# Two pairs of blocks by two levels in the feed-forward's first pass, a fourth block prepared in self-attention, and down prepared after gate and up

## The chip, the cores and the metric

One core of a Trainium2 chip runs the whole program. The metric is the device time of one execution in microseconds. Beside the times stands a profiled execution of the same program, from which every duration below is read.

## What is computed

A decoder layer in float32 on 16 batches of 128 rows and 1024 columns: self-attention with one head of 256, a linear cross-attention with eight heads of 64, and a gated feed-forward whose three weight matrices are stored as four-bit numbers with a scale and a zero for each group of 64.

```python
x = x + self_attention(layernorm(x), Wqkv, bqkv, Wo, bo)
x = x + cross_attention(layernorm(x), ctx, ctx, Wq, Wk, Wv, Wo, bo, g)
n = layernorm(x)
Wg, Wu, Wd = (dequantize(W_q, scale, zero) for each of gate, up, down)   # 2752x1024, 2752x1024, 1024x2752
h = silu(n @ Wg.T) * (n @ Wu.T)
x = x + h @ Wd.T
```

## The kernel before

**Products by seven instead of eight.** The feed-forward cuts each matrix product into 2x2 parts and makes it from seven products of sums and differences of the parts instead of eight (a scheme of the Strassen and Winograd kind). The numbers of the seven are 1 to 7. `GATE` gives their order in gate and up, `DOWN` in down and in the outer level. Products add into each other in PSUM: 6, 5 and 3 go on in the bank of 1, and 4 in that of 7, so a bank is read by another engine between two products that write it.

**Blocks.** The 2752 inner columns are cut into ten blocks of 2 x 128 and a last one (`RB`) of 2 x 96. The rows are cut into two passes of eight batches (`PASSES`); pass 0 is the first pass. In pass 0, `one_block` makes a block with one level: for gate and for up seven products of four matmuls, each 128x128 weights by 512 columns. A float32 matmul shows as two records in the profile, so a block has 2 x 7 x 4 x 2 = 112 records, on line 1087. `last_block` makes the last one. In pass 1, `two_levels` takes two blocks and gate and up together: seven outer products (`OUTERS`, in the order of `DOWN`), each made of seven inner products of four matmuls with 256 columns. A pair has 7 x 7 x 4 x 2 = 392 records, tile name `q`.

**What surrounds a product.** In `products`, ScalarE copies products 1, 7 and 6 out of PSUM (tile `k`), and `got` gives VectorE the readings after 2, 5, 4 and 3: in the gate half an addition and ScalarE's silu (tile `sg`), in the up half an addition and a multiplication (tile `h`). Product 3 writes the bank that `got((1, 1), ...)` has read after product 5; only product 4 lies between. In `two_levels`, VectorE makes the inner operands of the next outer product (`inner_right`, tile `ti`, four instructions of 128x512), GpSimd the inner weights (`inner_left`, tile `li`, four), and `got` adds the readings into `U`, `V` and `C` with one to three VectorE instructions each. After the outer products 2, 3, 7 and 4, `finish` has ScalarE take the silu and VectorE multiply twice (`h`). `soon_due` and `extra` are lists of such work that `do_extra` puts between the inner products. In pass 1 the operands that `KEPT` names are made once and kept for all five pairs.

**Weights.** `prepare` is a generator that turns four-bit weights into the seven operands of each matrix of a block: `load_raw` loads numbers and scales, VectorE makes float numbers (tile `pa`), combines them (tile `pc`), and SyncE stores seven tiles of 256 KB to DRAM. Each call of `next` is one step: first half of the matrix, second half, combinations; the matrix "r" of the last block has one step only. Loads run two halves ahead (one in self-attention). `EARLY` = 3 blocks of gate and up are prepared in self-attention, where the loop over the four groups of batches (t = 0 to 3) calls `next` six times in the middle of t = 1 and t = 2 and three times behind them. The rest is prepared beside the products of pass 0: `attention_done` builds the list of jobs once the last work of cross-attention is done, in block 0, and `beside`, called after each product, makes a step after nine of a block's fourteen products. Gate and up alternate in the list with down.

`load_weights` loads the operands back, two to a tile of the pool `cw`, four tiles ahead (`AHEAD`), in the order of `to_load`. Most transfers go through SyncE's queue, in program order where the code asks for it.

**Order.** `InOrder` wraps an engine and keeps its instructions in the order of the program; without it the scheduler may move an instruction. `tensor` and `vector` are such wrappers; `products` uses `nc.tensor` directly. Memory comes from pools that are opened and closed in stack order on a left and a right side; a tile waits for whatever lay there before.

**Before block 8** (`RB - 2`) the operands of pass 1 are loaded (`pass1`, eight transfers of 512 KB) into the pool `cxb`, which `attention_done` opens.

Of the kernel before, what the change touches and what calls it, by code (L numbers as in the profile page):

```python
# [18 lines left out]
P = 128  # L19
# [46 lines left out]
def decoder_layer(  # L66
# [215 lines left out]
    EARLY = 3  # L282
# [27 lines left out]
    with (  # L310
# [166 lines left out]
        for t in range(NT):  # L477
# [14 lines left out]
            for f in range(4):  # L492
# [9 lines left out]
                if more and t > 0:  # L502
                    for _ in range(1 + f % 2):
                        next(early, None)
# [457 lines left out]
    with ExitStack() as gs:  # L962
# [9 lines left out]
        def attention_done():  # L972

            nonlocal cxb, rest
            sides.close()
            prep_pools(second, "f", 6, 2)
            jobs = []
            for blk in range(EARLY, len(BLOCKS)):
                jobs += [(blk, mat) for mat in ("gu" if blk < RB else "rm")]
                if blk >= EARLY + 2:  # L980
                    jobs.append((blk - EARLY - 2, "d"))
            jobs += [(blk, "d") for blk in range(len(BLOCKS)) if (blk, "d") not in jobs]
            rest = prepare(jobs, 2, nc.sync, vector)
            banks.append(pool("c_u", 4, space=PSUM, side="right"))
            cxb = pool("c_xb", 1)
# [9 lines left out]
        def tiles_of(blk):  # L995
# [3 lines left out]
        OUTERS = [(i, q) for i in range(NI) for q in DOWN]  # L999
        to_load = deque(  # L1000
            [t for blk in range(len(BLOCKS)) for t in tiles_of(blk)]
            + [[(2 * i + f, mat, q) for mat in "gu"] for i, q in OUTERS for f in range(2)]
            + tiles_of(RB)
        )
# [65 lines left out]
        def products(T, got):  # L1070
# [7 lines left out]
            def product(q):  # L1078
# [7 lines left out]
                for j in range(JC):  # L1086
                    nc.tensor.matmul(  # L1087
# [20 lines left out]
        def one_block(blk, T, between):  # L1108
# [21 lines left out]
            make = {"g": products(T, gate), "u": products(T, up)}  # L1130
# [4 lines left out]
        def last_block(ps, T, between):  # L1135
# [24 lines left out]
            def half_product(p, w, q, start, stop):  # L1160
                for j in range(JC):
                    nc.tensor.matmul(  # L1162
# [63 lines left out]
        R = {}  # L1226

        def inner_right(T, q):

            if q in KEPT and (q, 7) in R:  # L1230
                return []

            def t(kc, h):
                return T[q][:, ts(kc, CHUNKS), ts(h, HT)]

            R[q, 1], R[q, 2], R[q, 3] = t(0, 0), t(1, 0), t(1, 1)

            def comb(k):
                if k == 5:
                    tag = KEPT.get(q, "ti")  # L1240
                    pool = {"ti": deep_pool, "X4": [xres]}.get(tag, [xlate])[0]
                    R[q] = pool.tile([P, 4, CHUNKS, HT], F32, name="ti", tag=tag, bufs=1)
                dst = R[q, k] = R[q][:, (5, 6, 7, 4).index(k)]
                a, b = {
                    5: (t(0, 1), t(0, 0)),
                    6: (t(1, 1), R.get((q, 5))),
                    7: (t(1, 1), t(0, 1)),
                    4: (t(1, 0), R.get((q, 6))),
                }[k]
                vector.tensor_tensor(dst, a, b, ALU.subtract)  # L1250

            return [lambda k=k: comb(k) for k in (5, 6, 7, 4)]

        def inner_left(L, pool, tag):
# [9 lines left out]
            def comb(k):  # L1264
                t = L[k] = pool.tile([P, 2, CHUNKS, P], F32, name="li", tag=tag)
# [10 lines left out]
        deep_pool = []  # L1276
        deep = ExitStack()

        def two_levels(T):
            scalar = InOrder(tc, nc.scalar)  # L1280
            deep_pool.append(
                deep.enter_context(
                    tc.tile_pool(name="c_d", bufs=1, side="right", reuse_waits="tile")
                )
            )
# [14 lines left out]
            def multiply(n, p):  # L1300
# [5 lines left out]
                ps = bank[set_]  # L1306
                for m in range(2):
                    for c in range(CHUNKS):
                        tensor.matmul(
                            ps[:, m, :],  # L1310
# [7 lines left out]
                if p in (1, 7, 6):  # L1318
# [3 lines left out]
                    scalar.copy(t, ps)  # L1322
# [28 lines left out]
            def finish(i, q):  # L1351
# [5 lines left out]
                def mult(f):  # L1357
# [4 lines left out]
                    if s == 1:  # L1362
                        store(2 * i + f, 4, half, t)
# [20 lines left out]
            def prepare_outer(n):  # L1384
                state[n] = {"L": {}, "bank": {}, "kept": {}}

                state[n]["left"] = inner_left(
                    state[n]["L"], *((chc, "hc") if n == 0 else (ct, "sg"))
                )
# [6 lines left out]
            for n, (i, q) in enumerate(OUTERS):  # L1396
                last = n + 1 == len(OUTERS)
                if q in (1, 5):
                    sums["U" if q == 1 else "V"] = deep_pool[0].tile(
# [9 lines left out]
                if q not in (1, 5):  # L1409
                    sums["C"] = deep_pool[0].tile(wide, F32, name="C")  # L1410
                if not last:
                    soon_due.extend(inner_right(T, OUTERS[n + 1][1]))
                if n == 0:
                    extra.append(lambda: outer_operand(T, 4))
                elif n == 4:
                    extra.extend(inner_right(T, 4))
# [20 lines left out]
                load_weights()  # L1437
                if not last:
                    do_extra(len(soon_due))
                    multiply(n + 1, 7)  # L1440
                if q in (2, 3, 7, 4):
                    finish(i, q)


                if q == 3:
# [9 lines left out]
                del state[n]  # L1455
            return extra
# [10 lines left out]

        for n in range(AHEAD):
# [4 lines left out]
        T1 = {}  # L1473

        def beside(n, mat, q):
# [4 lines left out]
            elif n % 7 in (0, 2, 4, 5) or n == 6:  # L1480
                next(rest, None)

            if blk == RB:
                for k in {("r", 0): (5,), ("r", 1): (7,), ("m", 6): (6,)}.get((mat, q), ()):
                    outer_operand(T1, k)
                if (mat, q) == ("m", 1):
                    for step in inner_right(T1, 1):
                        step()

        for blk in range(len(BLOCKS)):  # L1490
            if blk == RB - 2:
# [4 lines left out]
            if blk == RB:  # L1496
                blocks.update(pass1)
                last_block(0, T, beside)
            else:
                one_block(blk, T, beside)  # L1500
# [4 lines left out]
        remaining = two_levels(T1)  # L1505
# [272 lines left out]
```

## Time and profile before

| | us |
|---|---|
| median of three runs | 2297.44 (2296.18 to 2297.61) |
| the profiled execution, its own time | 2296.27 |
| its span, first to last instruction | 2294.5 |
| block 0's first product to the first of block 1 (with the end of cross-attention) | 808 to about 884 |
| blocks 1 to 9 of pass 0 | about 884 to 1317 |
| two levels in pass 1, five pairs | 1355 to 1780 |
| down | from 1818 |

The rows come from the page's span and from the chain of work that ended last. A row of the chain gives a start, a length and what ran, with x for the count of records. A row of the table by stretches gives the busy time of each engine with its number of instructions, the granted clock of TensorE as a share of full speed, the mean busy share of the 16 DMA engines (a little over 1 when they are full) and the rate. A row of single instructions gives start, length, engine, line, operation and tiles (out<-in), and in brackets how long the engine had been idle and what ended that. PE is TensorE's matmuls, PEld its weight loads, DVE VectorE, ACT ScalarE, POOL GpSimd, SP SyncE. Line 62 is the wrapper's, so tiles tell such instructions apart.

### The profile page before, as it was taken

The page shows a single profiled execution, that of the slowest core. Times are in us where ns is not written, and L with a number is a line of the kernel's source. Part 1 is how long each engine was busy: PE and PEld are TensorE (multiplying, and loading weights), DVE is VectorE, ACT ScalarE, POOL GpSimd, SP SyncE. Part 2 cuts the span into 40 slices and gives each one's busy share as a digit, 9 for nine tenths or more (in the row PEclk, how much of TensorE's full clock was granted, in tenths as well). Part 3 has the DMA queues.
Part 4 walks back from the last instruction along what each step waited for, and adds up shares of the span by engine and source line. Part 5 has one row for each costly group of instructions (what it writes and reads, how often), then busy time and mean ns, then how long its engine had stood idle before and what let it go on. Part 6 is the DMA issues. An engine that isn't in the chain of part 4 may idle for free.

```text
span 2294.5 us, 25166 instructions
## 1 busy us (share of the span) xinstructions
PE 2269.7 (99%) x8928; PEld 1581.6 (69%) x8928; DVE 1554.0 (68%) x2210; ACT 555.4 (24%) x887; POOL 389.2 (17%) x283
## 2 busy tenths in 40 slices
PE   8999999999999999999999999999999999999999
PEld 7556566666666664444444468888888588888888
DVE  6694788788788836677776548777777655444463
ACT  2111256665665652111111111222121100000000
POOL 5120122222222210000000024444443000000000
PEclk9999999999999999999999999999999999999999
DMA  6242356566576657888789733654654974434631
GB/s 245 62 138 90 110 156 184 164 193 189 161 229 203 171 157 249 264 273 281 260 282 332 256 104 103 202 173 140 202 183 145 328 243 153 140 125 148 221 115 37
DMA packets 274797, 425.19 MB, mean 185 GB/s; under 512 B 26225, under 2 KB 119793, under 8 KB 274545
## 3 DMA queue, kind: packets, MB, share of 16 engines
q1 hardware_dynamic: 254192, 396.06, 54.5%
q10 hardware_dynamic: 18016, 18.62, 2.6%
q0 software_dynamic: 2464, 8.91, 1.0%
q8 instruction: 71, 1.16, 0.2%
q14 instruction: 54, 0.43, 0.1%
HBM read 265.62 MB, written 157.35 MB: 184 GB/s over the span
## 4 chain that ended last, share of the span: by engine, by line
PE 94%; DVE 3%; DMA 1%; issue 1%; ACT 0%; SPq 0%; POOL 0%; DVEq 0%; POOLq 0%; ACTq 0%
PE p L1087 23%; PE po L1663 21%; PE q L62 18%; PE mm L62 11%; PE kq L62 8%; PE mm L392 5%; PE tr L62 3%; PE mm L407 2%; PE mm L288 2%; PE p L1162 1%; PE tr L339 1%; DMA kh<-kd 1%; DVE bnst L62 0%; DVE qden L62 0%; DMA wo_again<-in_wo 0%
## 5 line engine op out<-in xcount | busy, mean ns | idle before, releaser
L1087 PE MATMUL p<-b,w 128*128 128x512 f32 x704 | 310.4, 592 | 0.7 <-DMA w<-wg 0.7
L1087 PEld LDWEIGHTS p<-b,w 128*128 128x128 f32 x704 | 133.4, 190 | 167.1 <-issue 162.8
L1087 PE MATMUL p<-T,w 128*128 128x512 f32 x528 | 234.2, 592 | 0.0
L62 PE MATMUL q<-ti,li 128*128 128x256 f32 x840 | 193.0, 379 | 1.0 <-DVE ti L62 1.0
L1087 PEld LDWEIGHTS p<-T,w 128*128 128x128 f32 x528 | 100.1, 190 | 124.6 <-issue 123.1
L1663 PE MATMUL po<-wc,lc 128*128 128x256 f32 x840 | 183.4, 379 | 0.0
L62 POOL TENSOR_TENSOR li<-w 128x512 f32<-128x512 f32 x70 | 96.1, 1374 | 514.6 <-DMA w<-wu 476.8
L62 PEld LDWEIGHTS q<-ti,li 128*128 128x128 f32 x840 | 159.2, 190 | 23.8 <-issue 1.7
L1663 PEld LDWEIGHTS po<-wc,lc 128*128 128x128 f32 x840 | 159.6, 190 | 21.8
L708 POOL TENSOR_TENSOR qe<-qe,qden 128x1024 f32<-128x1024 f32 x64 | 121.6, 1900 | 266.3 <-DVE qden L62 233.6
L62 ACT COPY k<-q 128x512 f32<-128x512 f32 x105 | 61.4, 585 | 324.8 <-PE q L62 324.8
L62 DVE TENSOR_TENSOR pa<-pa,sz 128x512 f32<-128x512 int32 (+1 forms) x172 | 129.0, 750 | 5.4
L1663 PE MATMUL po<-wq,lq 128*128 128x256 f32 x560 | 126.7, 379 | 0.0
L62 PE MATMUL mm<-kh,cxt 128*128 128x256 f32 x512 | 123.0, 383 | 3.3 <-DMA kh<-kd 3.1
L62 PE MATMUL kq<-cx,wk_sb 128*128 128x512 f32 x256 | 122.0, 599 | 3.5 <-ACT ke L665 3.5
L62 PEld LDWEIGHTS mm<-qs,m_sb 128*128 128x128 f32 x512 | 97.2, 190 | 38.9 <-issue 28.0
L62 PE MATMUL kq<-wq_sb,xn 128*128 128x512 f32 x256 | 120.4, 593 | 0.0
L62 PE MATMUL mm<-qs,m_sb 128*128 128x256 f32 x512 | 120.3, 379 | 0.0
L62 PEld LDWEIGHTS mm<-kh,cxt 128*128 128x128 f32 x512 | 96.1, 190 | 33.6 <-issue 18.5
L62 DVE TENSOR_REDUCE qmx<-kq 128x16 f32<-128x1024 f32 x64 | 76.3, 1193 | 63.0 <-PE kq L62 62.8
L1663 PEld LDWEIGHTS po<-wq,lq 128*128 128x128 f32 x560 | 106.0, 190 | 15.7 <-issue 0.9
L392 PE MATMUL mm<-xnT,wqkv_sb 128*128 128x512 f32 (+1 forms) x320 | 113.2, 510 | 0.0
(189 smaller groups left out, 3651.9 us busy)
## 6 DMA issues: line engine op xcount, KB each, us to landing
w<-wu SPq DMA_DIRECT2D x140, 256.0 KB, 3.5
lq<-h SPq DMA_DIRECT2D x140, 256.0 KB, 4.4
w<-wg SPq DMA_DIRECT2D x138, 256.0 KB, 3.0
kd<-kt SPq DMA_DIRECT2D x64, 512.0 KB, 3.5
kh<-kd SPq DMA_DIRECT2D x128, 256.0 KB, 5.6
h<-hc SPq DMA_DIRECT2D x80, 256.0 KB, 2.8
wq<-wd SPq DMA_DIRECT2D x70, 256.0 KB, 5.0
h<-h SPq DMA_DIRECT2D x60, 256.0 KB, 3.2
```

The source lines that it names most:

```text
L62: return lambda *args, **kw: self._tc.keep_in_program_order(fn(*args, **kw))
L288: tensor.matmul(ps, oT[:, d, ts(b % BPT, S)], wo_d[d][:, ts(h, 512)], start=(d == 0), stop=(d == 1),)
L339: nc.tensor.transpose(tr[:, j, :], xn[:, ts(4 * h + j, P)], ident)
L392: nc.tensor.matmul(ps[:, tokens], wqkv_sb[:, f, c, :], xnT[:, c, tokens], start=(c == 0), stop=(c == CC - 1),)
L407: nc.tensor.matmul(ps, xnT[:, c, ts(i, S)], wqkv_sb[:, 4:6, c, :], start=(c == 0), stop=(c == CC - 1),)
L708: nc.gpsimd.tensor_tensor(qe, qe, den.unsqueeze(2).to_broadcast(wide), ALU.mult)
L1087: nc.tensor.matmul(ps, wt[:, j, :], T[q][:, j, :], start=(first == q and j == 0), stop=(q in (2, 3, 4) and j == JC - 1), skip_group_check= ...
L1162: nc.tensor.matmul(bank[p], w[:, j, :], T[q][:, j, :], start=(start and j == 0), stop=(stop and j == JC - 1), skip_group_check=True,)
L1663: nc.tensor.matmul(bank[:, i, :], l[:, ts(i, S)], w,  start=(start and c == 0 and i % 2 == 0), stop=(stop and c == len(pairs) - 1), skip_g ...
```

## The change

- `EARLY` becomes 4, and the six calls of `next` are made in t = 3 too.
- The list of jobs for the rest has gate and up of blocks 4 to 9 first, then four blocks of down, the last block's "m" and "r", then the other seven of down.
- `PAIRS = [2, 3]`: blocks 4 to 7 are made in pass 0 by `two_levels(0, ...)`, between block 3 and block 8; `to_load` follows. With `ps == 0` the function stores both h of a block as `one_block` does, keeps no operands for later pairs, and takes its tiles from a pool `c_d` that is opened before block 3 and closed after the stage. The operands for its first outer product are made in block 3.
- `beside` makes a step after twelve of fourteen products of a block, after five in the last block; in the stage a step follows the outer products 1, 2 and 5.
- `cxb` is opened, and the operands of pass 1 are loaded, after the stage.
- `products` and `half_product` use the wrapper `tensor`, but for block 0.

```diff
-    EARLY = 3
+    EARLY = 4
...
-                if more and t > 0:
+                if t > 0:
                     for _ in range(1 + f % 2):
                         next(early, None)
...
             prep_pools(second, "f", 6, 2)
-            jobs = []
-            for blk in range(EARLY, len(BLOCKS)):
-                jobs += [(blk, mat) for mat in ("gu" if blk < RB else "rm")]
-                if blk >= EARLY + 2:
-                    jobs.append((blk - EARLY - 2, "d"))
-            jobs += [(blk, "d") for blk in range(len(BLOCKS)) if (blk, "d") not in jobs]
+            jobs = [(blk, mat) for blk in range(EARLY, RB) for mat in "gu"]
+            down = [(blk, "d") for blk in range(len(BLOCKS))]
+            jobs += down[:4] + [(RB, "m"), (RB, "r")] + down[4:]
             rest = prepare(jobs, 2, nc.sync, vector)
             banks.append(pool("c_u", 4, space=PSUM, side="right"))
-            cxb = pool("c_xb", 1)
...
+        PAIRS = [2, 3]
+        order = [blk for blk in range(RB) if blk // 2 not in PAIRS]
+        order.insert(2 * PAIRS[0], None)
+        to_load = deque([t for blk in order[: 2 * PAIRS[0]] for t in tiles_of(blk)])
+        to_load += [t for i in PAIRS for t in tiles_of_pair(i)]
+        to_load += [t for blk in order[2 * PAIRS[0] + 1 :] + [RB] for t in tiles_of(blk)]
+        to_load += [t for i in range(NI) for t in tiles_of_pair(i)] + tiles_of(RB)
...
-        def products(T, got):
+        def products(T, got, tensor=tensor):
...
-                    nc.tensor.matmul(
+                    tensor.matmul(
...
+            engine = nc.tensor if blk == 0 else tensor
+            make = {"g": products(T, gate, engine), "u": products(T, up, engine)}
...
+        class Operands:
+            def __init__(self, T, kept):
+                self.T, self.kept, self.R, self.pool = T, kept, {}, None
...
+                        R[q] = pool.tile(
+                            [P, 4, CHUNKS, HT],
+                            F32,
+                            name="ti",
+                            tag=tag,
+                            bufs=1 if self.kept else 2,
+                        )
...
-        def two_levels(T):
+        def two_levels(ps, pairs, operands, between=lambda q: None):
...
+                    if ps == 0:
+                        store(2 * i + f, 1 + s, half, t)
+                    elif s == 1:
                         store(2 * i + f, 4, half, t)
...
+                do_extra(len(soon_due))
                 if not last:
-                    do_extra(len(soon_due))
                     multiply(n + 1, 7)
                 if q in (2, 3, 7, 4):
                     finish(i, q)
+                between(q)
...
-            elif n % 7 in (0, 2, 4, 5) or n == 6:
+            elif n % 7 != 3 and (blk < RB or n % 2 == 0):
                 next(rest, None)
+            if blk == 2 * PAIRS[0] - 1 and n == 9:
+                for step in first_operands.inner_right(DOWN[0]):
+                    step()
...
-        for blk in range(len(BLOCKS)):
-            if blk == RB - 2:
+        for blk in order:
+            if blk is None:
+                two_levels(
+                    0, PAIRS, first_operands, lambda q: q in (1, 2, 5) and next(rest, None)
+                )
+                deep.close()
+                cxb = pool("c_xb", 1)
                 pass1 = new_blocks(cxb, lambda k: f"b{k}")
                 for _ in block_loads(1, pass1):
                     pass
```

## The prediction

> **What bounds the kernel now.** I read the page's busy shares first, then the chain that ended last, then stretches of the second half, and last single instructions of the two-level stage.
>
> ```profile
> PE 2269.7 (99%) x8928; PEld 1581.6 (69%) x8928; DVE 1554.0 (68%) x2210; ACT 555.4 (24%) x887; POOL 389.2 (17%) x283
> ```
>
> TensorE is busy for 99%, so time can only come from fewer or shorter matmuls, and any wait put in front of a matmul is paid in full. The chain in order of time (start, length, what) shows what a matmul costs when nothing holds it up:
>
> ```profile
> 874.31 439.47 PE p L1087 x1024
> 1436.14 343.87 PE q L62 x1592
> ```
>
> One 512-column record of a one-level product costs 439.47/1024 = 0.4292 us, one 256-column record of a two-level product 343.87/1592 = 0.2160 us. Blocks 1 to 9 of the first pass run without one gap (112 records, 48.07 us each; block 1 starts near 884.4, block 8 near 1221), and so do four of the five pairs of the second pass. The same stretches by engine (columns: stretch, length, busy PE, PEld, DVE, ACT, POOL with instructions, PE clock, DMA share, GB/s):
>
> ```profile
> 200.00:220.00 20.00, 20.00 (x52) 9.54 (x51) 0.00 (x0) 2.06 (x3) 0.00 (x0) 1.00 0.28 102
> ...
> 881.00:929.00 48.00, 48.00 (x113) 21.28 (x112) 34.80 (x59) 7.29 (x11) 0.00 (x0) 1.00 0.84 273
> ...
> 1249.60:1257.60 8.00, 8.00 (x20) 3.61 (x19) 5.23 (x10) 1.17 (x2) 0.00 (x0) 1.00 1.04 256
> 1257.60:1265.60 8.00, 8.00 (x20) 3.47 (x19) 7.76 (x13) 0.00 (x0) 0.00 (x0) 1.00 1.05 347
> ```
>
> The clock is full throughout. VectorE has room in a block (34.80 of 48), none of its work lies in 200 to 220, and in block 8 the DMA engines are already full: over the nine slices of 8 us from 1217.6 to 1289.6 they moved 315, 405, 349, 364, 256, 347, 311, 370 and 358 GB/s, 342 on average, at shares of 0.99 to 1.05.
>
> **What is removed: 896 records become 784 shorter ones.** Two pairs are four blocks: 4 x 112 x 0.4292 = 192.3 us go. By two levels a pair is 7 x 7 products of four matmuls of two records, 392: 2 x 392 x 0.2160 = 169.3 us come. **-22.9 us.** Everything below is what may be given back.
>
> **The fourth early block.** A gate or up matrix is 16 VectorE instructions. In the first pass six of them (one step) take 3.58 us from start to start, the four combinations 2.53: 2 x 3.58 + 2.53 = 9.7 us a matrix, three steps. Two more matrices are 19.4 us. The early calls now run into the last group of four batches: there VectorE is empty from 199.5 to 222.1, under 27.5 us of query and key products (191 to 218.6), the first slice above. The SyncE queue issues 4 raw loads, 4 scale loads and 14 stores more; behind them wait the context loads issued at 201.9, first used after 257, and the loads that it issues at 244.5. Cost 0; without that cover it would be up to 19.4. ACT and GpSimd are not touched there.
>
> **Blocks 1 to 3: twelve steps instead of nine.** VectorE: 28.6 us of preparation for three matrices (tiles pa and pc in that stretch) become 38.1, plus the block's own 6.2: 44.3 of 48.07. The place that can bite: product 3 adds into the bank that `got` reads after product 5, with only product 4 (3.43 us) between. After the reading that follows product 4 come, on VectorE, step, step, then three more: in steady state I find that reading 0 to 1 us late, so 2.4 us are in hand. DMA: four matrices of 2.62 MB (4 raw or scale loads, 7 stores of 0.262), 3.67 of weights, 1.05 of h: 15.2 MB, and 15.7 with the 0.5 by which the measured stretch (13.1) exceeds its count: 327 GB/s against 342. Between 0 and 4 us; I take 1, as the same waits cost nothing at 273.
>
> **The two-level stage itself.** Its VectorE work: the page's forms on C, U, V and h sum to 229.1 us for five pairs, 45.8 a pair; combinations of operands are made anew each time, 28 x 0.78 (ti) = 21.8; three steps 9.7. That is 77.3 of 84.7 us. In the second pass most ti are kept, so its first pair shows the tight spot (start, length, engine, what):
>
> ```profile
> 1393.55 1.75 DVE L62 TENSOR_TENSOR ti<-T,ti 128x512 f32<-128x512 f32 x1
> ```
>
> ```profile
> 1393.12 1.64 POOL L62 TENSOR_TENSOR li<-w,li 128x512 f32<-128x512 f32 x1 [3.89 <-PE q L62]
> ```
>
> ```profile
> 1393.78 3.69 PE L62 MATMUL q<-ti,li 128*128 128x256 f32 x16 [0.81 <-DVE ti L62]
> ```
>
> After outer product 2, VectorE must multiply h twice (2.4 us), then do two readings and three ti before inner product 7 of the next outer: TensorE lost 0.81 us. And a VectorE instruction with both inputs in SBUF that meets a GpSimd one waits for it: 1.75 for 0.69. The change puts a 3.6 us step ahead of those h, behind which wait both readings and the ti. VectorE idles there for 2.6 us until ACT's silu, so 1 to 2.3 us come on top: 1.7 to 3.1. The second tight outer is 7: three instructions per reading, two h and now four ti. Its products in the trace have the matmul at 1430.8; its last needed reading ended at 1433.2 with the h 0.9 us later than it need be and no ti. Three ti of 0.6 put it at 1434.1, 3.3 late; if no GpSimd instruction is met, 1.4. The step after 1 and the combinations after 5 find VectorE idle for 5.1 and 4.6 us: 0. So per pair 3.1 to 6.4 us; met collisions could double the larger spots (1.07 each). Two pairs: 3 (if the silu wait covers all of the step) to 16; I take 2 per tight outer, **+8**, nearer to the low rows since in the trace most meetings were harmless. GpSimd's 56 li (1.37 us, 77 us) and ACT's copies lie beside it, as they do in the second pass.
>
> [...]
>
> **Blocks 8 and 9, where down is now prepared.** 73 steps are left (12 matrices of gate and up x 3, 11 of down x 3, 3 for m, 1 for r). Block 0 takes 3 (in the trace its first step comes after the twelfth product), blocks 1 to 3 take 36, the stage 6: block 8 has steps 46 to 57, which are d3, m, r, d4 and most of d5, block 9 58 to 69, down alone, and the last block the rest. A down matrix moves 3.41 MB (scales are 0.52 a half). Block 8, with loads two units ahead: 5.9 of loads, 7.1 of stores, 3.67, 1.05, and 4.19 of the second pass's x: 21.9 MB. Block 9: 5.9 + 7.3 + 3.6 + 1.05 = 17.9. About 4.1 MB may still be on the way at the end of it (two units of loads, four stores, three weight tiles). (39.8 - 4.1)/0.342 = 104.4 us against 96.1: 8.3 late. VectorE is in order, so a raw tile that is late holds the readings behind it, and TensorE after the 3.4 us of product 4: **+5**. At the fastest slice (405) it is 0; at the two slices quoted (302 on average, those with most down scales) it is 18.7. Now the nine slices show VectorE waiting 4.3 us for DMA in all, and TensorE not at all, with nine steps. SyncE issues about 94 transfers in block 9 at 0.5 us each (60 us for some 120 in those slices), so that queue is full too. It costs the same lateness, not a second one.
>
> [...]
>
> **The rest.** Products held in program order: in blocks 1 to 9 the trace has them in that order already, 0. Two new changes of stage (0 to 2 us; the one in the trace, 1354.8, has no gap): +0.5. Five steps in the last block: VectorE is busy for 16.1 of 41 us there, 17 more fit, 0.
>
> **Sum** against the profiled execution (2296.27, of which the span is 2294.5): -22.9 + 1 + 8 + 5 + 0.5 = -8.4, 2287.9. The median shown is 1.2 higher: **2289**.
>
> **Rivals.** *(a) All of it is hidden but 3 us in the stage:* -20, 2277.5. For it: no gap in blocks 8 and 9 now, at full DMA. Against: those blocks carry a third more. 0.15. *(b) VectorE and GpSimd eat the gain in the stage:* 5 us per tight outer, 20 instead of 8: 2301, within what counts as no change. For it: 91% of VectorE's time taken before any collision. Against: the five pairs of the second pass lost 1.7 us in all (425.0 us from 1354.98 to 1780.01, for 1960 x 0.2160 = 423.4). 0.2. *(c) DMA turns blocks 8 and 9 slower:* at 302 GB/s 18.7 instead of 5: 2303. It decides below 316 GB/s: there 35.7 MB take 112.9 us, 13.4 more than 96.1 + 3.4, which is what the other terms leave. For it: the two slices. Against: the mean of nine. 0.2, with the worse forms of (b) in it. **Forecast as summed:** 0.45.
>
> Two in a thousand (4.6 us) is about what a measurement of this kernel can tell from no change. Faster by more (below 2292.8): forecast and (a), 0.6. Within: (b), 0.2. Slower: (c), 0.2. The range reaches from (a) to (c): 2278 to 2303; the forecast's own is 2283 to 2295.
>
> **What would show it.** 784 records of line 1087 and 2744 of q; blocks 8 and 9 longer than 48.07 with VectorE waiting for raw or szd; in the stage waits of q for ti after outers 2 and 7, and 169.3 us plus them; blocks 1 to 3 at 48.1; VectorE busy from 200 to 220 with no longer self-attention. A stage below 173 us, or blocks 8 and 9 without a gap, would make the terms wrong; so would a wait at a place that I have at 0.

## The result and the profile after

The changed kernel takes **2317.28 us** (median of 7 executions, 2305.64 to 2318.36) beside 2296.18 us for the kernel before (7 executions on the same chip, 2294.36 to 2297.61): a ratio of **1.0075, 95% interval 1.0054 to 1.0097**. It is 0.75% slower. The prediction was 2289 us, faster, in a range from 2278 to 2303; the result lies outside it, on the other side. The profiled execution took 2317.28 us, its span 2315.5, against 2296.27 and 2294.5 before.

The page of the changed kernel, busy times and two of the groups (busy time and mean ns, then the idle time in front of them and who ended it):

```profile
PE 2263.5 (98%) x9264; PEld 1653.1 (71%) x9264; DVE 1678.3 (72%) x2340; ACT 564.9 (24%) x899; POOL 469.1 (20%) x339
...
L62 PE MATMUL q<-ti,li 128*128 128x256 f32 x1176 | 281.4, 391 | 17.4 <-DVE ti L62 17.4
...
L62 PE MATMUL p<-b,w 128*128 128x512 f32 x432 | 193.0, 599 | 5.4 <-DVE h L62 5.4
```

The 336 records more (8928 to 9264) are the 448 of 0.4292 us that went and the 784 of 0.2160 that came, as the working of the first step had them, 4 x 112 and 392 x 2; the 896 in that step's heading is a slip that entered no sum. TensorE is still busy for 98%, but it now waits, and those records that it does run are longer in the mean (391 ns instead of 379, 599 instead of 592). The waits of the changed kernel from 880 to 1420 us, from block 1 to some way into the second pass (engine, who is waited for, us in total, times, longest):

```profile
PE q L62 <- DVE ti L62: 17.2, 9, 3.4
PE p L62 <- DVE h L62: 5.4, 2, 3.5
PE q L62 <- DVE C L62: 1.8, 1, 1.8
PE q L62 <- DVE U L62: 1.5, 1, 1.5
```

All of them end on VectorE; two of the nine on ti, 0.83 and 0.82 us, lie in the second pass. By stretches of the changed kernel (the new stage; block 8; block 9; the last block and what of block 9 was late; columns as in the prediction):

```profile
1032.30:1233.60 201.30, 182.47 (x786) 155.44 (x785) 168.99 (x209) 32.49 (x51) 73.44 (x52) 0.94 0.45 147
1233.60:1281.60 48.00, 48.00 (x113) 21.24 (x112) 39.90 (x68) 7.06 (x11) 0.00 (x0) 1.00 0.98 322
1281.60:1329.60 48.00, 44.82 (x105) 19.57 (x103) 39.08 (x66) 5.97 (x10) 0.00 (x0) 0.99 1.05 336
1329.60:1373.90 44.30, 43.97 (x96) 19.40 (x97) 38.94 (x55) 3.98 (x7) 1.76 (x2) 0.93 0.80 252
```

Three things stand in the first line. The stage took 201.3 us for 169.3 us of matmuls. VectorE was busy for 169.0 us of it: as much as TensorE's matmuls take at the full clock, so a stage of the length that was counted left it no room at all. And the granted clock was 0.94, where it had been 1.00 in every stretch of the kernel before that the prediction looked at. Block 8 lost nothing; block 9 lost its time at one wait and in the slow clock behind it.

Put together, against the kernel before (us, from the start of the first product to the end): the first product starts 1.5 later; blocks 1 to 3 take 2.1 more; the stage takes 201.27 where 784 x 0.2160 = 169.34 were counted, **+31.9**; blocks 8 and 9 with the last block 140.4 instead of 133.9, +6.5; the second pass's stage +1.1; down +0.8. That is 43.9 given back against 22.9 gained: +21.0, the difference of the two profiled executions.

**Where the 31.9 lie.** The waits in the stage sum to 18.8 us: in the first pair 1.54 (on U, outer product 1), 2.36 (on ti, after 2), 2.27 (after 6), 0.84 (after 3) and 3.43 (after 7), in the second 1.77 (on C, in 6), 2.36 (after 6), 0.84 (after 3) and 3.43 (after 7). "After 6" stands for the wait ahead of inner product 7 of the outer product that follows 6. Most of the other 13 us are matmuls that ran slowly. TensorE's own timeline (start, length, what, idle before):

```profile
1062.65 5.23 PE L62 MATMUL q<-ti,li 128*128 128x256 f32 x16 [2.36 <-DVE ti L62]
...
1092.63 3.62 PE L62 MATMUL q<-ti,li 128*128 128x256 f32 x16
...
1121.61 6.45 PE L62 MATMUL q<-ti,li 128*128 128x256 f32 x16 [3.43 <-DVE ti L62]
```

Sixteen such records take 3.62 us with no wait ahead of them, 5.23 after one of 2.36 and 6.45 after one of 3.43. The granted clock in stretches of 3.41 us around the last of these shows it (the clock is the third figure from the end):

```profile
1116.96:1120.37 3.41, 1.22 (x6) 0.74 (x4) 3.34 (x5) 0.00 (x0) 1.26 (x1) 1.00 0.12 44
1120.37:1123.79 3.42, 2.18 (x5) 1.85 (x6) 2.89 (x5) 0.00 (x0) 0.00 (x0) 0.50 0.00 0
1123.79:1127.20 3.41, 3.41 (x9) 2.70 (x8) 0.23 (x1) 1.54 (x2) 1.27 (x1) 0.50 0.00 0
1127.20:1130.61 3.41, 3.41 (x17) 2.97 (x16) 1.82 (x4) 0.59 (x1) 1.26 (x1) 1.00 0.43 159
```

TensorE was busy for 1.22 us of the first stretch; the clock is 0.50 in the whole of the next, again in the one after it, and back at 1.00 in the fourth. The stage has seven such stretches, block 9 two. A stretch of 3.41 us at half speed costs 1.71 us where TensorE is busy for all of it; less the idle time that falls into them, the seven cost 10.8 us. Some 2 us lie in the records beside the nine waits: a record lasts 0.38 us, though the next one of an unbroken row starts 0.2160 us after it, so a wait costs 0.16 us more than its idle time, and the first records behind it run a little longer.

**Why VectorE was late.** In the prediction a step takes 3.58 us. The first one in the stage, put after outer product 1 (VectorE and then GpSimd, both of the changed kernel):

```profile
1048.26 1.49 DVE L62 TENSOR_SCALAR pa<-raw 128x512 int32<-128x512 int32 x1
1049.77 2.37 DVE L62 TENSOR_TENSOR pa<-pa,szd 128x512 f32<-128x512 int32 x2
1052.06 1.49 DVE L62 TENSOR_SCALAR pa<-raw 128x512 int32<-128x512 int32 x1
1053.58 1.42 DVE L62 TENSOR_TENSOR pa<-pa,szd 128x512 f32<-128x512 int32 x2
...
1060.76 1.75 DVE L62 TENSOR_TENSOR ti<-T 128x512 f32<-128x512 f32 x1
```

```profile
1048.18 1.27 POOL L62 TENSOR_TENSOR li<-w,li 128x512 f32<-128x512 f32 x1 [5.21 <-PE q L62]
1049.92 3.35 POOL L62 TENSOR_TENSOR li<-w 128x512 f32<-128x512 f32 x2 [0.46 <-PE q L62]
...
1060.44 1.52 POOL L62 TENSOR_TENSOR li<-w,li 128x512 f32<-128x512 f32 x1 [4.01 <-PE q L62]
```

The step met three combinations of GpSimd: an instruction of 0.42 us took 1.49 twice, a pair of 1.42 took 2.37, and the step 6.7 us instead of 3.58. The next step began with the same instruction, with no GpSimd one beside it:

```profile
1063.63 0.41 DVE L62 TENSOR_SCALAR pa<-raw 128x512 int32<-128x512 int32 x1
```

In the whole stage 41 of VectorE's 209 instructions took over 0.2 us longer than the shortest of their kind, 38 us in all, and every one of them ran beside a GpSimd instruction; the 14 that read q out of PSUM beside one took no longer than the others of their kind, at most 0.69 us. Nothing waited for the first step at its place. But the readings of the next outer product's banks and its ti queue behind it on VectorE, one ti met GpSimd once more (1.75 for 0.68), and the matmuls that need it began 2.36 us late.

### The profile page after: what moved, and what is told of

Its sections match the earlier page's. It is cut to its first block, busy times and chain, and to the rows that moved or that the text cites. A ratio compares the mean times of both kernels' runs of the same rounds, so it can differ in the third digit from the quotient of the medians.

```text
span 2315.5 us, 26157 instructions
## 1 busy us (share of the span) xinstructions
PE 2263.5 (98%) x9264; PEld 1653.1 (71%) x9264; DVE 1678.3 (72%) x2340; ACT 564.9 (24%) x899; POOL 469.1 (20%) x339
## 5 line engine op out<-in xcount | busy, mean ns | idle before, releaser
L62 PE MATMUL q<-ti,li 128*128 128x256 f32 x1176 | 281.4, 391 | 17.4 <-DVE ti L62 17.4
L62 PEld LDWEIGHTS q<-ti,li 128*128 128x128 f32 x1176 | 230.0, 196 | 54.6 <-issue 13.2
L62 POOL TENSOR_TENSOR li<-w 128x512 f32<-128x512 f32 x98 | 135.2, 1381 | 374.2 <-DMA w<-wu 296.7
L62 ACT COPY k<-q 128x512 f32<-128x512 f32 x147 | 86.1, 585 | 499.6 <-PE q L62 499.6
L62 PE MATMUL p<-b,w 128*128 128x512 f32 x432 | 193.0, 599 | 5.4 <-DVE h L62 5.4
L62 PEld LDWEIGHTS p<-b,w 128*128 128x128 f32 x432 | 83.0, 193 | 110.2 <-issue 99.5
L62 PE MATMUL p<-T,w 128*128 128x512 f32 x304 | 134.7, 592 | 0.0
L62 PEld LDWEIGHTS p<-T,w 128*128 128x128 f32 x304 | 57.8, 190 | 72.7 <-issue 71.7
```

Source lines behind the costliest of these rows:

```text
L62: return lambda *args, **kw: self._tc.keep_in_program_order(fn(*args, **kw))
```

## The experiments

Two theories stood at the start. **V:** the stage loses its time because VectorE is late, and the clock falls because TensorE waits. **D:** the moved steps and their transfers cost time wherever they lie. Ratios are to the kernel before on the same chip, with 95% intervals. "The last three blocks" are 8, 9 and the last one, 133.91 us before. The length of a stage and its waits come from the one profiled execution of each kernel. In experiment 6 the changed stage, with the same nine waits, took 197.1 us instead of 201.3, as four stretches of half clock fell into it and not seven. So a difference of about 4 us between two stages says little.

**1. No steps in the stage.** The weights of down for blocks 1 and 2 are not prepared; those of block 0 take their place.

```
-            jobs += down[:4] + [(RB, "m"), (RB, "r")] + down[4:]
+            jobs += [down[0], down[3]] + [(RB, "m"), (RB, "r")] + down[4:]
...
-                    0, PAIRS, first_operands, lambda q: q in (1, 2, 5) and next(rest, None)
+                    0, PAIRS, first_operands, lambda q: None
```

> The changed kernel without the six preparation steps in the two-level stage of the first pass: down of blocks 1 and 2 is not prepared, and block 0's is used in its place. Everything else stands. Theory V (VectorE is late in the stage; TensorE waits 18.8 us there for ti, U and C, and the granted clock halves after the waits over 2 us, 13 us more): the waits in the outer products 1, 2 and 6 go (9 of 18.8 us), those in 3 and 7 stay (0.84 and 3.43 us, twice), so the stage falls from 201 us to about 185, the whole to about 2301. Theory D (twelve steps a block and the transfers moved with them cost the time, wherever they lie): the stage may shorten by a few us, the whole stays above 2312.

Measured: 2298.21 us, ratio 1.0005 (0.9995 to 1.0015). The stage took 185.2 us, as theory V had it. The waits after 2 and 6 are gone; the 1.55 on U, which the expectation had among those that go, 0.82 after 3 and 3.44 after 7 stay in place. So the six steps, 19.4 us of VectorE's work by the prediction's rows, cost some 16 of the stage's 31.9 us, and the steps are not all of it.

**2. No combinations of operands in the stage.** The four ti of the first outer product stand in for those of all others, 52 VectorE instructions fewer; the steps stay.

```
+                if not self.kept and (DOWN[0], 4) in R:
+                    for k in (5, 6, 7, 4):
+                        R[q, k] = R[DOWN[0], k]
+                    return []
```

> The changed kernel with the inner operands ti made for the first outer product of the stage alone; the other thirteen use the same tile, so 52 VectorE instructions are left out. The six steps stay. Theory V: no wait for ti is left and the readings are 2.4 us earlier in each outer product; the stage comes down from 201 us to 170 to 174, the clock stays full there, the whole is 2317 - 28 = about 2289, block 9 still losing its 6.5. Theory D: above 2310, since steps and transfers are unchanged.

Measured: 2286.95 us, ratio 0.996 (0.9945 to 0.9975), the stage 172.0 us. Its line, to be held against the first one of the table above:

```profile
1031.30:1203.30 172.00, 169.68 (x781) 147.90 (x780) 126.22 (x156) 32.46 (x51) 71.13 (x52) 1.00 0.53 170
```

With 126 instead of 169 us of VectorE's work, the steps left in place, the waits shrink to 1.16 us twice and the clock stays at 1.00. So it is not the steps as such. Nor is it VectorE's total: with 132 us of work the stage of experiment 1 still took 185.2. What counts is the work that VectorE has right ahead of the matmuls that wait, and the ti are a part of that. The GpSimd meetings go down with it (27 us instead of 38); no experiment took away the meetings and left the work, so how the lateness divides between the two stays open.

**3. The other parts of the change without the stage.** The early fourth block, the order and the twelve steps a block alone.

```
-        PAIRS = [2, 3]
-        order = [blk for blk in range(RB) if blk // 2 not in PAIRS]
-        order.insert(2 * PAIRS[0], None)
+        order = list(range(RB))
+        order.insert(RB - 2, None)
```

> The changed kernel without the two-level stage: all ten blocks of the first pass are made by one level, with the fourth block prepared early, gate and up ahead of down, twelve steps a block, and the second pass's operands loaded before block 8 as they were. Theory V: TensorE's work is that of the kernel before; the parts cost 1.5 us ahead of block 1, some 2 in the blocks with twelve steps and nothing in blocks 8 and 9, where the list has run out: 2298 to 2302. Theory D: they cost what the change lost and more: above 2310.

A miss: 2310.41 us, ratio 1.0059 (1.0039 to 1.0078). Blocks with twelve steps of gate and up cost nothing (first line below), and neither did block 4, the first in which down is prepared by such steps (48.07 us). But block 5 took 52.17 us, with a wait of 2.25, and block 6 57.97, with waits of 3.17 and 3.02, each wait with a stretch of half clock behind it (the other two lines); in block 7 the list has run out:

```profile
950.00:998.00 48.00, 48.00 (x113) 21.23 (x112) 44.17 (x75) 6.01 (x10) 0.00 (x0) 1.00 0.97 322
...
1098.00:1149.00 51.00, 49.91 (x112) 21.84 (x112) 42.31 (x72) 5.48 (x10) 0.00 (x0) 0.97 1.03 325
1149.00:1200.00 51.00, 45.77 (x99) 20.03 (x100) 29.57 (x49) 5.99 (x11) 0.00 (x0) 0.93 0.95 307
```

VectorE's own waits from 1046 to 1185 us say what it was late for:

```profile
DVE pa L62 <- DMA szd<-in_dsz: 13.3, 10, 2.1
DVE pa L62 <- DMA raw<-in_dq: 3.6, 3, 2.2
```

By blocks, the waits of pa for these two loads are 2.1 us in block 4, 6.0 in 5 and 8.9 in 6: the loads fall behind by and by. So preparing down at this pace over several blocks has a price of its own, 14 us in all here, slow clock included. Of the parts tried in this run, theory D holds for this one alone.

**4. The ti for inner product 7 made first.** In the changed kernel it comes third of four, though product 7 is the first that needs one.

```
+                order = (5, 6, 7, 4) if self.kept else (7, 5, 6, 4)
...
-                return [lambda k=k: comb(k) for k in (5, 6, 7, 4)]
+                return [lambda k=k: comb(k) for k in order]
```

> The changed kernel with one order changed: in the first pass's two-level stage VectorE makes the operand for inner product 7 first of the four ti and not third, since TensorE needs it first. Nothing is left out. Theory V: the waits of 2.3 to 3.4 us shrink by 1.2 us or more (two ti of 0.6 us), product 6 then waits up to 1.7; most waits fall below the 1.8 us under which the clock of the changed kernel never fell, so most of the 13 us of slow clock go too: stage about 182 us, the whole 2295 to 2302. Theory D: no change, 2317. If the clock fell for another reason than waits (all engines busy at once), the stage shortens by the waits alone, to about 192, with the clock still down in it: 2308.

Measured: 2302.06 us, ratio 1.0022 (1.0013 to 1.0032), the stage 184.9 us instead of 201.3 with the same work (168 us of VectorE) in another order. The 3.43 after 7 became 2.65 and 1.72; new waits on C (2.59, 1.75) come up. What counts is when VectorE is late, not only how much it does.

**5. The kernel before with useless work on VectorE.** At outer product 5 of the second pass, 14, 6, 8, 10 and 12 subtractions are added for the five pairs, so that TensorE waits and has nothing else to do differently.

```
+                if q == 5:
...
+                    for _ in range((14, 6, 8, 10, 12)[i]):
+                        vector.tensor_tensor(spare, T[2][:, 0], T[2][:, 1], ALU.subtract)
```

> The kernel before, whose TensorE never waits long in the second pass, with subtractions of 128x512 (0.6 us each) that nobody uses put on VectorE ahead of the readings of outer product 5: 14, 6, 8, 10 and 12 of them in the five pairs. VectorE idles 3.4 us there and has some 2 us more in hand, so TensorE should wait about 3 to 5, 0, 1, 2 and 3 us. Theory W (the granted clock halves after a wait of some 2 us or more, whatever caused it): the clock falls after the waits over 2 us and not after the shorter ones, each fall costs 1.5 to 3 us more, and the whole is 2296 + 10 to 13 of waits + 5 to 9 = 2311 to 2318. Theory L (the clock falls because VectorE, GpSimd and TensorE are all loaded, as they are in the changed kernel's stage): the clock stays at 0.999, and the whole is 2306 to 2309.

Measured: 2332.02 us, ratio 1.0159 (1.0142 to 1.0176). The waits were larger than expected, 24.9 us in all, so the time lies above the 2311 to 2318, and the stage was 37.1 us longer: most of the other 12 us are half clock. The wait of 1.58 us brought no slow clock, at the same place of the program. Waits of 2.36 and 3.04 us were followed by one stretch of 3.41 us at 0.50, 4.49 and 5.94 by two, 7.07 by three. So waits of 2.36 us and more brought the clock down; that all engines are loaded is not needed, since it fell in block 9 of the changed kernel too, where GpSimd did nothing (0.00 in the row above).

**6. The scales of down loaded once.** The first ones stand in for all; each of the other units has up to four loads fewer.

```
...
-            for g in range(w // 32):
+            for g in range(0 if again else w // 32):
```

> The changed kernel with the scales and zeros of down loaded once and used for every half of every block: 0.52 MB and four issues fewer for each half, VectorE's work unchanged. Theory T (blocks 8 and 9 are late for lack of transfers): block 9 moves 13.7 MB and not 17.9, the wait of 3.5 us and the slow clock behind it go, blocks 8, 9 and the last one take 134 us and not 140.4, the whole 2317 - 6 = 2311 or, with the clock of a better execution, 2300 to 2306. Theory S (twelve steps fill VectorE): they still take 138 to 141 us. The two-level stage is unchanged in both.

Measured: 2303.05 us, ratio 1.0038 (1.0023 to 1.0053). The last three blocks took 133.90 us, their time before, and block 9 has no wait; the stage keeps every one of its waits. In the changed kernel VectorE waited for these loads from block 8's start to the end of block 9:

```profile
DVE pa L62 <- DMA szd<-in_dsz: 8.5, 6, 1.9
```

That settles block 9: its 6.5 us come from transfers, not from VectorE's own work. Whether by their bytes or by their number in SyncE's queue is not told apart, as both went down.

**7. Experiment 4 with the steps after 1, 5 and 4.**

```
-                    0, PAIRS, first_operands, lambda q: q in (1, 2, 5) and next(rest, None)
+                    0, PAIRS, first_operands, lambda q: q in (1, 5, 4) and next(rest, None)
```

> The operand for product 7 made first, as in e4, and the stage's steps after the outer products 1, 5 and 4 in place of 1, 2 and 5. Nothing is left out. Theory V: with the step gone from ahead of the two h in outer product 6, its waits (2.6 and 1.8 us in e4) go; after 4 comes outer product 1 with three readings only, so no new wait; those in 7 (2.7 and 1.7) stay. Stage 175 to 178 us against 184.9 in e4, the whole 2288 to 2296. If the steps cost the same wherever they lie in the stage: 2300.

Measured: 2301.24 us, ratio 1.0023 (1.0014 to 1.0032); the stage 182.9 us, 5 above the expectation, and the whole is nearer to the 2300 of the other reading. The waits on C in outer product 6 went, as expected, but 1.55 on U and four of 0.64 on ScalarE's copies came. Moving steps within the stage brought 2 us at most, and block 9 had a wait of 5.55 us this time. That the units on their way when it begins had changed may be the reason; no run shows it.

**8. The two pairs in turn.** For each outer product first one pair, then the other, so that its ti are made once for both, half as many; eight steps in the stage, ten in each of blocks 8 and 9, seven in the last block.

```
+            if ps == 0:
+                OUTERS = [(i, q) for q in DOWN for i in pairs]
...
+                    if i == pairs[0]:
+                        todo_right = operands.inner_right(DOWN[DOWN.index(q) + 1])
+                        soon_due.extend(todo_right[:2])
+                    else:
+                        soon_due.extend(todo_right[2:])
```

> A version meant to beat both. The stage takes each outer product for both pairs in turn, so each ti is made once for the two (28 VectorE instructions instead of 56), two in each turn and 7 first; eight steps lie where no h is due; blocks 8 and 9 make ten steps each, the last block seven. Nothing is left out. Theory V: stage 169.5 to 173 us, no wait over 1.8 us in it and a full clock, blocks 8, 9 and last 134 to 136 us, the whole 2275 to 2282. If the loss has another cause than VectorE's lateness: above 2290.

A miss: 2297.17 us, ratio 1.0008 (0.9999 to 1.0018), instead of 2275 to 2282. The stage took 176.9 us (4 over the expectation: 1.94 on U with a slow stretch, 1.34 twice on ACT), blocks 8 and 9 ran through. But the last block lost 9.81 us at one wait, with three stretches of half clock, and the second pass's stage 4.6 us. VectorE stood idle ahead of the first:

```profile
1329.99 0.43 DVE L62 TENSOR_SCALAR pa<-raw 128x512 int32<-128x512 int32 x1 [9.34 <-DMA wd<-pa]
```

and SyncE's queue, which has to store pa before VectorE may write it again, stood behind another store:

```profile
SPq L1040 <- DMA sg<-sg: 16.9, 1, 16.9
```

So a step in the last block cost 9.81 us here, because it needed that queue before the sg transfer had landed. It is a third way in which a moved step costs time, beside VectorE's load and the DMA engines'.

**9 and 10. The same with the steps put where VectorE has room,** and with two steps more in the stage, after (2, 7) and (3, 3), instead of in blocks 8 and 9. A pair of numbers is the pair of blocks and the outer product that a step comes after; SKIP lists the products of a block that have no step.

```
-        SKIP = {3: (3, 9, 10), 8: (1, 3, 8, 10), 9: (1, 3, 8, 10), RB: (3, 7)}
+        SKIP = {3: (3, 9, 10, 12, 13), 8: (3, 8, 10), 9: (3, 8, 10), RB: (1, 3, 5, 7)}
...
-                    0, PAIRS, first_operands, lambda k: k in ((2, 1), (3, 1), (2, 6), (3, 6), (2, 5), (3, 5), (3, 7), (2, 4)) and next(rest, None)
+                    0, PAIRS, first_operands, lambda k: k in ((2, 1), (3, 1), (2, 6), (3, 6), (2, 5), (3, 5), (3, 7), (2, 4), (2, 2), (3, 2)) and next(rest, None)
```

> The pairs in turn as before (one set of ti for both), with the steps put where VectorE has room: none after the last two products of block 3, ten in the stage, eleven in each of blocks 8 and 9, five in the last block as in the changed kernel. Theory V (VectorE's lateness, and the slow clock behind it, is all that the change lost): the U wait at the stage's start goes, the stage takes 171 to 174 us, blocks 8, 9 and the last block 133.9 to 135, the second pass's stage 425, and the time is 2275 to 2282 us. Theory D (the moved steps and transfers cost on their own, wherever they lie): blocks 8, 9 and the last block keep 5 us or more, and the time stays above 2287 us.

> As the run before it, but with twelve steps in the stage, the two more of them after outer product 7 of the first pair and 3 of the second, where VectorE has the last sums and two multiplications to do, and ten in each of blocks 8 and 9. Theory V: waits of 1 to 3 us for each of the two, and, where one is over 2.2 us, 1.5 to 3 us of slow clock; the stage takes 174 to 180 us and the time is 2279 to 2288 us. Theory D: blocks 8 and 9 have two steps and their transfers less, so the time is no longer than that of the run before it.

Measured: 2290.87 us, ratio 0.9977 (0.9968 to 0.9987), and 2294.84 us, 0.9996 (0.9987 to 1.0005). The first missed its 2275 to 2282: the stage took 177.0 us (1.99 on C with a slow stretch), the last three blocks 136.0, and the second pass's stage 432.1 instead of 425, since VectorE came into it with combinations left over (1.95 on U, 1.30 on ti, two slow stretches). The second has two steps fewer in blocks 8 and 9 and was not faster there (136.0 as well; in both, blocks 8 and 9 take 48.07 us each and the last block has a wait of 1.9), while its stage took 182.2 us with new waits on C of 2.32 and 1.75: theory D falls for ten or eleven steps a block, and V's price for two steps (1 to 3 us each) holds, with the stage 2 us above its range.

**11. The last fix.** One step more in block 3, none after outer product 2 of the second pair, twelve in block 8, four in the last block.

```
-        SKIP = {3: (3, 9, 10, 12, 13), 8: (3, 8, 10), 9: (3, 8, 10), RB: (1, 3, 5, 7)}
+        SKIP = {3: (3, 9, 10, 13), 9: (3, 8, 10), RB: (1, 3, 5, 7, 8)}
```

> As the pairs in turn with the steps spread, but one step more in block 3, none after outer product 2 of the second pair, twelve in block 8, and four instead of five in the last block, so that its last combinations are done before the second stage begins. Theory V: the waits on C in the stage and on U and ti at the start of the second stage go with the slow clock behind them (3 and 7 us there), the stage takes 172 to 174 us, the second pass's stage 425 to 426, and the time is 2278 to 2284 us. Theory D: block 8 with its twelve steps loses 3 us or more to transfers, and the time stays above 2288 us.

Measured: **2281.05 us** (2278.71 to 2282.68, 5 executions), ratio **0.9937 (0.9923 to 0.995)** to the kernel before, 36 us below the changed kernel. The second pass's stage took 426.3 us, the last three blocks 133.90, the stage itself 175.0 (1 above the expectation). TensorE's waits in this kernel from 880 to 1420 us, from block 1 to some way into the second pass:

```profile
PE q L62 <- ACT k L62: 2.7, 2, 1.3
PE q L62 <- DVE ti L62: 2.0, 3, 1.0
PE q L62 <- DVE C L62: 1.8, 1, 1.8
```

and its stage and block 8:

```profile
1026.90:1201.90 175.00, 170.57 (x785) 148.21 (x784) 150.29 (x189) 32.43 (x51) 73.62 (x54) 1.00 0.53 172
1201.90:1249.90 48.00, 48.00 (x113) 21.29 (x113) 39.92 (x68) 7.05 (x11) 0.00 (x0) 1.00 1.02 348
```

No wait is long enough to bring the clock down, and block 8 with its twelve steps lost nothing. This kernel keeps the change's idea and gets 17.6 of its 22.9 us by the profiled executions (2278.71 against 2296.27), of which the one of this kernel is its fastest; by the medians it is 14.8.

## Why the prediction was wrong

**The removed work: right.** The counts of records are as predicted, and a record still takes 0.2160 us where the clock is full: the 17.6 us of experiment 11 are that gain, less 5.3 given back.

**The step that failed: "The two-level stage itself", +8.** It measured +31.9, 23.9 more, in three parts:

- The spots that the step named. The h of outer product 2 are multiplied during 6, so its first spot, behind the step after outer product 2, is what is called "after 6" above: 2.27 and 2.36 us. Its second, after 7, measured 3.43 twice. That is 11.5 us, inside its own bounds (3.1 to 6.4 a pair, so 6.2 to 12.8); the 8 that it took, "nearer to the low rows", was 3.5 too low.
- The places that it had at 0. "The step after 1 and the combinations after 5 find VectorE idle ... 0." VectorE was idle in those places in the trace of before, but the first step put there took 6.7 us instead of 3.58 beside GpSimd, and 7.3 us of waits came at places without a price. The 2.36 after 2 in the first pair and the 1.77 on C in the second went with the steps (experiment 1). The 1.54 on U is lateness that came over from block 3, where VectorE still combined weights up to 1044.1 us: with no step after that block's last two products it is gone (experiment 9, beside 8). In the second pair, where VectorE was not late in this way, the step after 1 took 6.8 us and no wait followed it. The last two are 0.84 after 3, where the second pass of the kernel before lost 0.18.

  The stage was costed spot by spot, each with its own slack, though the sum on the page said there was hardly any: 77.3 us of VectorE's work for 84.7. It measured 84.5 a pair (169.0 for two). The 77.3 held some meetings already, since its rows are those of the second pass of the kernel before, where 74 of 405 instructions ran long beside a GpSimd one; that 91% of the time was taken "before any collision", as rival (b) has it, is not so. Without any meeting the work of the changed stage would be about 65 us a pair (169.0 less 38, for two). VectorE, in order and as full as the TensorE that it feeds (169.0 us of work beside 169.3), carried its lateness from spot to spot, as the 1.54 on U shows. Experiments 1 (132 us of work, 185 us of stage), 2 (126, 172) and 11 (150, 175) show that both the load and its place count.
- The granted clock. No term of the sum had it: 10.8 us in the stage, 2.7 in block 9. (The last 2.3 of the 31.9 lie beside the waits, as said above.) "The clock is full throughout" holds for the stretches that the prediction read, but the trace of before had one wait of over 2 us, in cross-attention, and a half clock behind it, which was there to be read:

```profile
699.00 2.40 PE L62 MATMUL mm<-kh,cxt 128*128 128x256 f32 x8 [2.16 <-DMA kh<-kd]
...
700.39:703.80 3.41, 3.41 (x7) 1.69 (x6) 1.16 (x2) 0.00 (x0) 0.00 (x0) 0.50 1.07 396
```

Experiment 5 shows, with waits of graded length, that they bring it about: from 2.36 us on there, and not at 1.58.

**"Blocks 1 to 3", +1:** 2.1, one wait of 1.85 us on h at the end of block 3. With the same twelve steps but without the stage, whose first four ti are made in block 3, that block took 48.06 us (experiment 3); the term counted no ti there. **"Blocks 8 and 9", +5:** 6.5, for the cause that it named, late loads for down (experiment 6); that the size came out so near is luck, as 3.5 of it is the wait and 2.7 the clock, which no term had. (In the nine slices of the kernel before that this step read, SyncE's queue issued 104 transfers, not some 120.) Experiment 3 shows the same mechanism where twelve steps of down fall into several blocks in a row. **"The fourth early block", 0,** cannot be told from the +1.5 with which the first product starts: in the ten experiments with the early block that start lies between 806.2 and 812.9 us, on both sides of the 808.0 before; in experiment 5, where the attention is that of the kernel before, it is 805.3. **"The rest", +0.5:** 1.9 in the second pass and down.

With the measured terms in place of its own the sum is 2287.9 + 1.1 + 23.9 + 1.5 + 2.9 = 2317.3.

**The rivals.** (b), VectorE and GpSimd eat the gain in the stage, was the mechanism, with 20 us as its price and a fifth of the chance; it too stopped at the waits, 18.8 us in all. (c), DMA in blocks 8 and 9, was priced at 18.7 and is worth 6.5. The rates in blocks 8 and 9 were 322 and 336 GB/s, below the 342 that the step took from the rows, and what came late were the small loads of scales, so the wait of 3.51 us in block 9 says nothing for or against that rate.

The executions of the changed kernel spread as the clock does: 2305.64 us at a mean granted clock of 0.998, 2317.28 at 0.993. Nine stretches at half speed, as in the stage and block 9 of the profile, take 9 x 1.71 = 15.4 us, 0.0066 of the span, which is nearly all that 0.993 lacks. This is in keeping with the last section: the same waits may or may not bring the clock down, by where they fall.

## What to carry to other kernels

When two engines feed one another in order, add up the whole stage before looking for slack spot by spot: at 91%, on an engine whose instructions stretch by 1 us when they meet another's (0.42 to 1.49 and 0.68 to 1.75 us here), plan on no slack, and take work away (shared operands) rather than move it. A stall of TensorE had two prices here, the wait and the clock behind it, so one wait of 3.4 us with two slow stretches behind it, as after outer product 7, cost about as much as seven of 0.84. And a moved step must be followed through every queue: VectorE's load, the loads and stores it issues, and what the stores stand behind.

## What was not expected of the hardware

The half clock came in whole stretches of **3.41 us on a fixed grid**: in the changed kernel it begins at 1062.35, 1079.41, 1120.37, 1178.40, 1219.36 and 1328.59 us, for 3.413 us (three times) or 6.827, and the later ones lie 5.00, 17.00, 34.00, 46.00 and 78.00 times 3.413 us after the first. In the changed kernel and all eleven experiments, from block 1 on, the clock fell after each full-speed stretch of the grid in which TensorE idled for 1.94 us or more (34 of them) and after none with 1.93 or less (13 lie between 1.5 and 1.93). The ends of matmuls are modelled, so the second decimal is not certain. A wait that the grid cut in two cost nothing more when both parts stayed below: 3.31 us in experiment 1 was cut into 1.93 and 1.37, and 2.09 in experiment 7 into 1.58 and 0.51. Once at half, a further 0.78 us of idle time kept the clock there for another stretch, and 0.50 or less let it return. So here a wait under 1.9 us cost itself, one of 2 to 3 us about 1.5 to 1.7 more if the grid did not cut it, and those of 3.4 to 3.7 us 1.5 to 3.0 more.

The bound is one of these matmuls. Near 250 us, among matmuls of 128 columns in self-attention, the clock fell in four experiments (1, 6, 7 and 10) after stretches with 1.14 to 1.72 us of idle time, and it did not in four others after 1.20 to 1.46, nor in the kernel before after 1.58 in the stretch from 290.79 us. Why it fell there stays open.
